# One stream for both stages of a bidirectional scan layer, with two changes of order, in a four-layer Trainium2 kernel

## The chip, the core and the metric

The kernel runs on one core of a Trainium2 chip. A core has five engines that run their own instruction queues and meet at semaphores: TensorE (PE, matmuls; its weight loads are listed as PEld), VectorE (DVE), ScalarE (ACT), GpSimd (POOL) and SyncE (SP, which here only issues DMA transfers). Each engine takes its instructions in program order. The metric is the device time of one execution in microseconds.

## The reference, cut to what matters

Four layers follow one another on an image batch of 8 x 64 x 64 x 64 in float32. Layer 1 and layer 3 are built on selective scans, and they are the ones that the change touches. Layer 3 is this:

```python
def mamba1(x, nw, ipw, cw, cb, xpw, dtw, dtb, Alog, Dp, opw):
    xn = rms_norm(x, nw)
    xz = xn @ ipw.T
    xc, z = (xz[..., :d], xz[..., d:])          # d = 256
    xc = silu(causal_dwconv(xc, cw, cb))
    dbl = xc @ xpw.T                            # 4 + 16 + 16 columns
    dt = softplus(dbl[..., :r] @ dtw.T + dtb)
    Bm, Cm = dbl[..., r:r + n], dbl[..., r + n:r + 2 * n]
    A = -exp(Alog)
    y = selective_scan(xc, dt, Bm, Cm, A)       # h = exp(dt A) h + dt x B;  y = sum_n h C
    y = (y + Dp * xc) * silu(z)
    return y @ opw.T

xt = mamba_bidir(xt, P, 0, 1) @ tlin_w + tlin_b + xt     # stage 0: along one image axis
xf = mamba_bidir(xf, P, 2, 3) @ flin_w + flin_b + xf     # stage 1: along the other axis
```

mamba_bidir runs mamba1 forward and on the reversed sequence with two sets of weights. A stage works on sequences of 64 positions, 16 states (n) and 256 channels (d). Stage 1 reads what stage 0 wrote, transposed. Layer 1 has the same recurrence in four directions with 128 channels.

## The kernel before, in words

**Tiles.** Layer 3 works in steps. A step is 8 sequences of 64 tokens in one direction: 512 tokens by 256 channels, held as tiles of 128 x 1024 (two halves of 128 channels side by side). Four groups g by two directions k are a chunk c of 8 steps, and 16 chunks (two per image, NB = 8 images) are a stage. So a stage has 128 steps of 16 states, 2048 scans.

**The stream** (`stream`, L433 to L579) is one loop over all the steps and states i of a stage. For each state, ACT makes `dA` = exp(dt A) (`decay`, L491), POOL makes `hb` = du B (`multiply_b`, L484), DVE runs the scan (L500), then DVE, or POOL for the "shared" states (5 or 4 of the 16), multiplies with C (`multiply_c`, L514), and PE adds the result into the accumulator `acc` with an identity matmul (`gather`, L306). The numbers `ahead` say how many states ahead the loads of B, the products hb and the loads of C are issued: (6, 3, 6) in layers 2 and 3, (5, 2, 3) in layer 1. In layer 3 (and 2) B and C of a state come as one tile `bc` and `fetch_c` does nothing. In layer 1 they come as two tiles from two pools of 4 (B) and 5 (C) buffers, and `fetch` (B) and `fetch_c` (C) both issue on SP's queue, B first (L543, L544). A load waits in that queue until its buffer is free: B's until POOL has made the hb that read it, C's until the product with C has been made.

**Beside the stream** run hand-ordered pieces. `prepare` of the next step is a generator of which one piece is taken per state: convolution and input projection on PE, Silu to `u`, a projection to dt, B and C (`dbl`), softplus to `dt` (L415), `du` = dt u on POOL (L2001), z's projection on PE (L2004), and then, on ACT, in this order: a copy that writes 1e30 into dt at one end of every sequence (L2015, so that exp(dt A) is 0 and the state starts anew), and z's Silu (L2017). The copy must come after POOL has read dt for du. `drain` (L2030) multiplies acc by z once a step's states are in. `finish` (L2046 to L2066) makes the output of a group: five matmuls, an ACT evacuation to `out`, and at an image's end (stage 0) or a chunk's end (stage 1) a store.

`begin` (L1884 to L1935) brings in a chunk. It loads `raw` twice (both 64-partition halves hold the same tokens, the lower one a position later), squares half of it at a time on ACT (L1900), averages on PE, copies the row to `ms` (L1906), sends it by DMA to `rs` spread over partitions (L1908), takes root and reciprocal, sends that to DRAM and back as `inv` in all partitions, and multiplies `xn` = raw inv on POOL (L1930). It is started by `done` of the first step of the chunk before, as a background task (`behind`) that advances one piece per state.

**Stages.** `layer3` calls `l3_stage` twice. Each call opens its own pools, issues 18 weight loads of its stage on SP, builds the products that the steps use (taps, w_z, w_end, w_res, skip, minus exp of A), clears raw and inv on POOL, runs `begin(0)` to its end, and then runs its own stream of 128 steps. `sq` is a tile of 64 x 1024 and `ms` one of 1 x 1024, each with one buffer. z's weights `w_z` lie in partitions 0 to 63.

Of the kernel before, what the change touches and what calls it, by code (L numbers as in the profile page):

```python
# [268 lines left out]
class Net:  # L269
# [163 lines left out]
    def stream(self, pools, ahead, steps, behind, rest=None):  # L433
# [1384 lines left out]
    def l3_stage(self, s, src, dst):  # L1818
# [5 lines left out]
        W, H = 512, 512 // HW  # L1824
        with ExitStack() as ctx:
            pool = lambda n, b, **k: ctx.enter_context(tc.tile_pool(name=f"l3{s}{n}", bufs=b, **k))
# [5 lines left out]
            def stage(name):  # L1832

                w = self.d["l3_" + name][:, 2 * s : 2 * s + 2]
                t = cp.tile(list(w.shape), F32, name="w_" + name)
                nc.sync.dma_start(t, w)
                return t

            linb = self.load(cp, "l3_linb")
            nw, w_in, cb, xp, dtw, dtb, A, D, w_out = (  # L1840
                stage(n) for n in ("nw", "in", "cb", "xp", "dtw", "dtb", "A", "D", "out")
            )
            lin = stage_lin = cp.tile([C, 2, C], F32, name="w_lin")
            nc.sync.dma_start(stage_lin, self.d["l3_lin"][:, s])
            self.minus_exp(A)
            nc.vector.tensor_scalar(A, A, -1e-27, None, ALU.min)
            skip = [self.diag(cp, f"skip{k}", D[:, k, :], 2) for k in range(2)]


            taps = [cp.tile([128, 2, 256], F32, name=f"taps{k}") for k in range(2)]  # L1850
            w_z = cp.tile([C, 2, 256], F32, name="w_z")
            w_end = cp.tile([128, 2, 2, C], F32, name="w_end")
            for k in range(2):
                for m in range(2):
                    for r in range(2):
                        row = self.d["l3_taps"][2 * s + k, m, r : r + 1, :]
                        nc.sync.dma_start(taps[k][r * C : r * C + C, m, :], row.to_broadcast([C, 256]))
                for m in range(2):
                    nc.vector.scalar_tensor_tensor(
                        taps[k][:, m, :], w_in[:, k, :256], nw[:, k : k + 1], taps[k][:, m, :], ALU.mult, ALU.mult  # L1860
                    )
                nc.vector.tensor_scalar(w_z[:, k, :], w_in[:C, k, 256:], nw[:C, k : k + 1], None, ALU.mult)

                for j in range(2):
                    ps = pp.tile([128, T], F32, name="mm")
                    nc.tensor.matmul(ps[:, :C], w_out[:, k, j * 128 : j * 128 + 128], lin[:, k, :], start=True, stop=True)
                    nc.scalar.copy(w_end[:, k, j, :], ps[:, :C])
            w_res = cp.tile([C, C], F32, name="w_res")
            nc.vector.tensor_tensor(w_res, lin[:, 0, :], lin[:, 1, :], ALU.add)
            nc.vector.tensor_tensor(w_res, w_res, self.ident[:C, :C], ALU.add)  # L1870
# [3 lines left out]
            nc.vector.memset(endless, 1e30)  # L1874

# [8 lines left out]
            def begin(c):  # L1884
# [4 lines left out]
                hold = chunks[c] = {"x": x}  # L1889
                from_ = src[q, rows, part * 4 * W : (part + 1) * 4 * W].rearrange("p (s t) -> p s t", t=HW)  # L1890
# [5 lines left out]
                for j in range(2):  # L1896
                    yield CALM_FREE
                    sq = p1.tile([C, T], F32, name="sq")
                    o = sq.rearrange("p (s t) -> p s t", t=HW)
                    nc.scalar.activation(o, x[:C, j * 2 * H : (j + 1) * 2 * H, ends[0]], AF.Square)  # L1900
# [4 lines left out]
                    ms = p1.tile([1, T], F32, name="ms")  # L1905
# [33 lines left out]
            class Step:  # L1939
# [6 lines left out]
                def __init__(self, c, g, k):  # L1946
                    self.c, self.g, self.k, self.rev = c, g, k, k == 1
                    self.shared = (2, 6, 10, 14) if k and g % 2 else (1, 4, 7, 10, 13)
                    self.lanes = [(slice(j * W, j * W + W), A[:, k, j, :]) for j in range(2)]

                def ready(self):

                    while begun.get(self.c) in behind:
                        net.advance(behind)

                def prepare(self):
                    k, hold = self.k, chunks[self.c]
# [6 lines left out]
                    for j in range(2):  # L1964
                        for m, f in enumerate((4, 6) if k else (3, 1)):
                            nc.tensor.matmul(  # L1966
                                tokens(px[:, j * W : j * W + W]),
                                taps[k][:, m, j * 128 : j * 128 + 128],
# [7 lines left out]
                    for j in range(2):  # L1976
                        at = slice(j * W, j * W + W)
                        nc.scalar.activation(u[:, at], px[:, at], AF.Silu, bias=cb[:, k, j : j + 1])  # L1978
                    pd = pp.tile([128, T], F32, name="mm")[:36, :W]
                    for j in range(2):  # L1980
                        nc.tensor.matmul(pd, xp[:, k, j, :], u[:, j * W : j * W + W], start=j == 0, stop=j == 1)  # L1981
# [7 lines left out]
                    for j in range(2):  # L1989
                        nc.tensor.matmul(  # L1990
                            pt[:, j * W : j * W + W], dtw[:, k, j * 128 : j * 128 + 128], dbl[0:4], start=True, stop=True
# [4 lines left out]
                    for j in range(2):  # L1996
                        at = slice(j * W, j * W + W)
                        net.softplus_act(dt[:, at], pt[:, at], dtb[:, k, j : j + 1])
# [13 lines left out]
                    yield CALM  # L2012

                    at = HW - 1 if k else 0
                    nc.scalar.copy(dt.rearrange("p (s t) -> p s t", t=HW)[:, :, at], endless)  # L2015
                    z = self.z = p2.tile([128, T], F32, name=f"z{k}")
                    nc.scalar.activation(z, pz, AF.Silu)  # L2017
# [5 lines left out]
                def skip(self, acc):  # L2023
                    for j in range(2):
                        at = slice(j * W, j * W + W)
                        nc.tensor.matmul(acc[:, at], skip[self.k][:, j, :], self.u[:, at], start=True, stop=False)
                    return True

                def drain(self, acc):
                    nc.vector.tensor_tensor(self.z, acc, self.z, ALU.mult)  # L2030
                    chunks[self.c][f"y{self.k}"] = self.z

                def done(self):
                    c, g = self.c, self.g
# [6 lines left out]
            def finish(c, g, ys):  # L2041
# [3 lines left out]
                x = chunks[c]["x"][:C, g * H : g * H + H, ends[0]]  # L2045
                nc.tensor.matmul(ps.rearrange("p (s t) -> p s t", t=HW), w_res, x, start=True, stop=False)  # L2046
                for k in range(2):
                    for j in range(2):
                        nc.tensor.matmul(  # L2049
                            ps, w_end[:, k, j, :], ys[k][:, j * W : j * W + W], start=False, stop=k == 1 and j == 1  # L2050
# [5 lines left out]
                if first:  # L2056
                    images[b] = p1.tile([C, L if s == 0 else 4 * W], F32, name="out")
# [10 lines left out]
            net = self  # L2068
# [30 lines left out]
```

## Time and profile before

| | us |
|---|---|
| timed runs, median of 3 | 24834.52 |
| timed runs, lowest to highest | 24824.01 to 24847.65 |
| profiled execution | 24819.55 |
| its span, first to last instruction | 24817.8 |

The profile is that of one execution. It reports for each engine when it was busy, and what released it where it waited. Over the span PE is busy 85%, DVE 90%, ACT 60% and POOL 89%, at a mean granted clock of TensorE of 0.940. The layers lie one after another in it:

| stretch, from the timeline | us |
|---|---|
| layer 1, first to last load of B for its stream | 1223.1 to 8458.4 |
| layer 2, first to last load of B and C for its scan | 8947.7 to 10596.2 |
| layer 3, first load to first scan's start | 11453.2 to 11520.9 |
| stage 0, first to last scan's start | 11520.9 to 18122.4 |
| stage 1, first to last scan's start | 18202.5 to 24800.8 |

The durations of the instructions that matter, from the page's groups: hb 2.36 us on POOL (L484), the scan 2.28 us on DVE (L500), the product with C 1.22 us on DVE and 2.36 us on POOL (L514), dA 0.69 us per half on ACT (L491), a switch of ACT's function table 1.28 us. "Idle before <-X" names the instruction that ended an engine's wait.

### The profile page before, as it was taken

To read this page: it belongs to the slowest core of one execution; us is meant where nothing else is said; L and a number is where in the kernel's file an instruction comes from. 1 tells how busy PE (TensorE), PEld (TensorE's weight loads), DVE (VectorE), ACT (ScalarE), POOL (GpSimd) and SP (SyncE) were. 2 spreads that over 40 slices of the span, in tenths; PEclk is the share of its full clock that TensorE was granted. 3 is DMA by queue.
4 is the path that set the end of the run, shared out by engine and by line. 5 is a ranking of instruction groups with operands and counts; after the bars stand their busy time and mean duration, and the time that the engine had idled before them with its cause. 6 is when DMAs were issued, how large, how long until landed. Compare 5 with 4: busy or idle time off the path is not lost. (4 is left out here: it accounts for less than half of the span.)

```text
span 24817.8 us, 193238 instructions
## 1 busy us (share of the span) xinstructions
PE 21209.1 (85%) x53146; PEld 8277.5 (33%) x53146; DVE 22437.6 (90%) x12958; ACT 14770.8 (60%) x18827; POOL 22097.5 (89%) x10583
## 2 busy tenths in 40 slices
PE   8877888888888888888888888888878888888888
PEld 6522333333333323322333333333323333333333
DVE  5399999999999679978999999999989999999999
ACT  4355555555555456624666666666666666666666
POOL 0199999999999669977999999999989999999999
PEclk9889999999999999999999999999989999999999
DMA  2399899899889669933455555555545554555454
GB/s 65 88 324 326 310 320 319 310 319 318 313 315 317 225 224 344 339 87 98 168 172 169 173 169 171 169 173 170 168 156 173 168 173 167 173 168 174 168 173 158
DMA packets 1835374, 5282.70 MB, mean 213 GB/s; under 512 B 533792, under 2 KB 540004, under 8 KB 1831984
## 3 DMA queue, kind: packets, MB, share of 16 engines
q1 hardware_dynamic: 1809712, 5207.00, 61.9%
q10 hardware_dynamic: 24576, 63.33, 0.7%
q8 instruction: 423, 6.93, 0.1%
q14 instruction: 663, 5.43, 0.1%
HBM read 5112.85 MB, written 156.11 MB: 212 GB/s over the span
## 5 line engine op out<-in xcount | busy, mean ns | idle before, releaser
L484 POOL TENSOR_TENSOR hb<-du,bc 128x1024 f32<-128x1024 f32 x4608 | 10745.6, 2359 | 201.3 <-DVE h L500 142.5
L306 PE MATMUL acc<-hc,ident 128*128 128x512 f32 x18560 | 8793.2, 615 | 109.8 <-DVE img L1266 61.4
L491 ACT ACTIVATE dA<-dt,w_A 128x512 f32<-128x512 f32 x8192 | 5655.4, 691 | 3950.7 <-DVE hc L514 2884.6
L500 DVE TENSOR_TENSOR_SCAN dA<-dA,hb 128x1024 f32<-128x1024 f32 x3320 | 7578.5, 2283 | 227.9 <-ACT dA L491 151.0
L306 PE MATMUL acc<-h,ident 128*128 128x512 f32 x8064 | 4623.7, 702 | 2390.1 <-POOL h L514 2361.7
L306 PEld LDWEIGHTS acc<-hc,ident 128*128 128x128 f32 x18560 | 3641.3, 200 | 5245.3 <-issue 4558.1
L484 POOL TENSOR_TENSOR hb<-du,b 128x1024 f32<-128x1024 f32 x2048 | 4837.5, 2395 | 460.4 <-DVE dA L500 220.7
L514 DVE TENSOR_TENSOR hc<-dA,bc 128x1024 f32<-128x1024 f32 x3232 | 3956.3, 1224 | 245.6 <-issue 5.8
L491 ACT ACTIVATE dA<-dt,w_l_A 128x1024 f32<-128x1024 f32 x2560 | 2857.1, 1117 | 1002.4 <-DVE hc L514 762.6
L500 DVE TENSOR_TENSOR_SCAN h<-dA,hb 128x1024 f32<-128x1024 f32 x1416 | 3229.2, 2280 | 148.2 <-ACT dA L491 144.8
L306 PEld LDWEIGHTS acc<-h,ident 128*128 128x128 f32 x8064 | 1560.4, 211 | 5100.2 <-POOL h L514 3403.4
L514 POOL TENSOR_TENSOR h<-h,bc 128x1024 f32<-128x1024 f32 x1376 | 3242.3, 2356 | 14.2 <-DVE h L500 14.2
L500 DVE TENSOR_TENSOR_SCAN dA<-dA,carry,hb 128x1024 f32<-128x1024 f32 x1320 | 3093.1, 2343 | 83.2 <-ACT dA L491 31.1
L514 DVE TENSOR_TENSOR hc<-dA,c 128x1024 f32<-128x1024 f32 x1408 | 1723.5, 1224 | 141.9 <-DMA c<-bc 32.0
L514 POOL TENSOR_TENSOR h<-h,c 128x1024 f32<-128x1024 f32 x640 | 1521.6, 2378 | 9.5 <-ACT carry L1249 8.9
L491 ACT ACT_TABLE_LOAD x1126 | 1444.7, 1283 | 20.0
L500 DVE TENSOR_TENSOR_SCAN h<-dA,carry,hb 128x1024 f32<-128x1024 f32 x600 | 1404.5, 2341 | 31.8 <-ACT dA L491 22.0
L1249 ACT COPY carry<-dA 128x1 f32<-128x1 f32 x1056 | 167.6, 159 | 1675.2 <-DVE hc L514 1635.5
L1966 PE MATMUL mm<-xn,taps 128*128 128x512 f32 x2048 | 939.1, 600 | 34.3 <-POOL xn L1930 31.1
L721 POOL MEMSET xf<- 128x24 f32 x33 | 4.3, 142 | 857.0 <-PE ps L742 728.0
L2001 POOL TENSOR_TENSOR du<-dt,u 128x1024 f32<-128x1024 f32 x256 | 602.8, 2355 | 18.5 <-ACT dt L415 18.5
L1981 PE MATMUL mm<-u,w_xp 128*36 128x512 f32 x1024 | 489.8, 601 | 149.2 <-ACT u L1978 140.1
(320 smaller groups left out, 18515.0 us busy)
## 6 DMA issues: line engine op xcount, KB each, us to landing
bc<-bc SPq DMA_DIRECT2D x4096, 512.0 KB
b<-bc SPq DMA_DIRECT2D x2048, 512.0 KB
c<-bc SPq DMA_DIRECT2D x2048, 512.0 KB
bc<-bc SPq DMA_DIRECT2D x512, 1024.0 KB
tmp<-rs SPq DMA_DIRECT2D x93, 512.0 KB
raw<-x SPq DMA_DIRECT2D x64, 512.0 KB
inv<-rs SPq DMA_DIRECT2D x64, 512.0 KB
tmp<-x SPq DMA_DIRECT2D x192, 128.0 KB
```

The source lines that it names most:

```text
L306: self.nc.tensor.matmul(o, lhsT, r, start=start, stop=stop)
L484: nc.gpsimd.tensor_tensor(s.shaped(hb[i]), s.shaped(s.du), B.pop(i), ALU.mult)
L491: nc.scalar.activation(dA[i][:, cut], s.dt[:, cut], AF.Exp, scale=A[:, n : n + 1])
L500: nc.vector.tensor_tensor_scan(h[:, way], dA[i][:, way], hb.pop(i)[:, way], s.first(n), ALU.mult, ALU.add)
L514: engine.tensor_tensor(s.shaped(o), s.shaped(h), CC.pop(i), ALU.mult)
L721: nc.gpsimd.memset(x[:, :, HW:], 0.0)
L1249: nc.scalar.copy(self.carry[:, n : n + 1], h[:, last : last + 1])
L1966: nc.tensor.matmul(tokens(px[:, j * W : j * W + W]), taps[k][:, m, j * 128 : j * 128 + 128], xn[:, :, f : f + HW], start=m == 0, stop=m == 1,)
L1981: nc.tensor.matmul(pd, xp[:, k, j, :], u[:, j * W : j * W + W], start=j == 0, stop=j == 1)
L2001: nc.gpsimd.tensor_tensor(du, dt, u, ALU.mult)
```

## The change

Three edits, cut to their core. The first is in `stream` and takes effect where B and C have their own pools, that is in layer 1:

```diff
             need(i + ahead[1], "du")
+            fetch_c(i + ahead[2])
             fetch(i + ahead[0])
-            fetch_c(i + ahead[2])
             multiply_b(i + ahead[1])
```

The second is at the end of `prepare`, with the weights of z now in partitions 64 to 127:

```diff
                         nc.tensor.matmul(
                             tokens(pz[:, j * W : j * W + W]),
-                            w_z[:, k, j * 128 : j * 128 + 128],
-                            xn[:C, :, 3 : 3 + HW],
+                            w.z[:, k, j * 128 : j * 128 + 128],
+                            xn[C:, :, 4 : 4 + HW],
...
                     yield CALM
+                    z = self.z = p2.tile([128, T], F32, name=f"z{k}")
+                    nc.scalar.activation(z, pz, AF.Silu)
 
                     at = HW - 1 if k else 0
                     nc.scalar.copy(dt.rearrange("p (s t) -> p s t", t=HW)[:, :, at], endless)
-                    z = self.z = p2.tile([128, T], F32, name=f"z{k}")
-                    nc.scalar.activation(z, pz, AF.Silu)
```

The third makes `layer3` one function with one set of pools. A class `Weights` holds a stage's weights; `load` issues its 18 loads (in this order: out, lin, nw, in, 8 of taps, cb, xp, dtw, dtb, A, D), of which w_in, w_out and lin go into two buffers of the stream's pool `bc` (they are read only while building), and `build` makes the products. Steps, chunks and `finish` carry the stage s as well, and read their weights from `weights[s]`, their input from `srcs[s]` and their output from `dsts[s]`:

```diff
     def layer3(self, src, dst):
-        self.l3_stage(0, src, self.hbm["x4"])
-        self.l3_stage(1, self.hbm["x4"], dst)
+        srcs, dsts = (src, self.hbm["x4"]), (self.hbm["x4"], dst)
...
+                def load(self):
+                    spare = pools[0].tile([128, 2, W], F32, name="bc")
+                    self.w_in = pools[0].tile([128, 2, W], F32, name="bc")
+                    self.w_out = self.take("out", spare[:C, 0, :].rearrange("p (k t) -> p k t", k=2))
+                    self.lin = spare[:C, 1, : 2 * C].rearrange("p (k t) -> p k t", k=2)
+                    nc.sync.dma_start(self.lin, net.d["l3_lin"][:, s])
+                    self.nw = self.take("nw")
+                    self.take("in", self.w_in)
...
                 for j in range(2):
                     yield CALM_FREE
-                    sq = p1.tile([C, T], F32, name="sq")
+                    both = p1.tile([128, T], F32, name="sq")
+                    sq, ms = both[:C], both[C : C + 1]
...
                     if self.k == 1:
-                        net.urgent.append(Task(finish(c, g, [chunks[c]["y0"], chunks[c]["y1"]])))
-                    if self.k == 0 and g == 0 and c + 1 < 2 * NB:
-                        begun[c + 1] = Task(begin(c + 1))
-                        behind.append(begun[c + 1])
+                        net.urgent.append(Task(finish(self.s, self.c, self.g, [hold["y0"], hold["y1"]])))
+                    more = self.s * 2 * NB + self.c + 1
+                    if self.k == 0 and self.g == 0 and more < 4 * NB:
+                        at = divmod(more, 2 * NB)
+                        begun[at] = Task(begin(*at))
+                        behind.append(begun[at])
...
             with tc.manual_schedule():
-                Task(begin(0)).run()
-                steps = [Step(c, g, k) for c in range(2 * NB) for g in range(4) for k in range(2)]
+                first = Task(begin(0, 0))
+                first.step()
+                weights[0].load()
+                weights[0].build()
+                first.run()
+                weights[1].load()
+                weights[1].build()
+                steps = [
+                    Step(s, c, g, k) for s in range(2) for c in range(2 * NB) for g in range(4) for k in range(2)
+                ]
                 self.stream(pools, (6, 3, 6), steps, behind)
```

In `build`, the four products for w_end go into one PSUM tile with one copy, where there were four of each; the rest is the same work per stage, now once for each stage before the one stream. `first.step()` issues the loads of raw for the first chunk ahead of the weights. What the last stage does at its end is as before.

More of the change, by code (lines that the diff above doesn't have):

```diff
@@ L1814, in layer3 @@
     def layer3(self, src, dst):
-        self.l3_stage(0, src, self.hbm["x4"])
-        self.l3_stage(1, self.hbm["x4"], dst)
-    def l3_stage(self, s, src, dst):
         nc, tc = self.nc, self.tc
         W, H = 512, 512 // HW
+        srcs, dsts = (src, self.hbm["x4"]), (self.hbm["x4"], dst)
         with ExitStack() as ctx:
-            pool = lambda n, b, **k: ctx.enter_context(tc.tile_pool(name=f"l3{s}{n}", bufs=b, **k))
+            pool = lambda n, b, **k: ctx.enter_context(tc.tile_pool(name="l3" + n, bufs=b, **k))
             cp, p1, p2 = pool("c", 1), pool("p1", 1), pool("p2", 2)
@@ L1830, in l3_stage @@
             hp = pool("h3", 3, space=DRAM)
[L1832 to L1837, printed above, removed]
-            linb = self.load(cp, "l3_linb")
[L1840 to L1870, printed above, removed]
+            linb = self.load(cp, "l3_linb")
             mean = cp.tile([C, 1], F32, name="mean")
@@ L1874, in l3_stage, with __init__, take, build @@
             nc.vector.memset(endless, 1e30)
+            class Weights:
+                def __init__(self, s):
+                    self.s = s
+                def take(self, name, t=None):
+                    w = net.d["l3_" + name][:, 2 * self.s : 2 * self.s + 2]
+                    if t is None:
+                        t = cp.tile(list(w.shape), F32, name=f"w_{name}{self.s}")
+                    nc.sync.dma_start(t, w)
+                    return t
+                def load(self):
+                    s = self.s
+                    spare = pools[0].tile([128, 2, W], F32, name="bc")
[5 more added lines that the diff above has]
+                    self.take("in", self.w_in)
+                    self.taps = [cp.tile([128, 2, 256], F32, name=f"taps{s}{k}") for k in range(2)]
+                    for k in range(2):
+                        for m in range(2):
+                            for r in range(2):
+                                row = net.d["l3_taps"][2 * s + k, m, r : r + 1, :]
+                                nc.sync.dma_start(self.taps[k][r * C : r * C + C, m, :], row.to_broadcast([C, 256]))
+                    self.cb, self.xp = self.take("cb"), self.take("xp")
+                    both = cp.tile([128, 2, 256], F32, name=f"both{s}")
+                    self.dtw, self.z = self.take("dtw", both[:4]), both[C:]
+                    self.dtb, self.A, self.D = self.take("dtb"), self.take("A"), self.take("D")
+                def build(self):
+                    s = self.s
+                    ps = pools[5].tile([128, T], F32, name="acc")[:, : 4 * C]
+                    for i in range(4):
+                        k, j = divmod(i, 2)
+                        nc.tensor.matmul(
+                            ps[:, i * C : i * C + C],
+                            self.w_out[:, k, j * 128 : j * 128 + 128],
+                            self.lin[:, k, :],
+                            start=True,
+                            stop=True,
+                        )
+                    self.end = cp.tile([128, 2, 2, C], F32, name=f"w_end{s}")
+                    nc.scalar.copy(self.end.rearrange("p k j o -> p (k j o)"), ps)
+                    for k in range(2):
+                        for m in range(2):
+                            nc.vector.scalar_tensor_tensor(
+                                self.taps[k][:, m, :],
+                                self.w_in[:, k, :256],
+                                self.nw[:, k : k + 1],
+                                self.taps[k][:, m, :],
+                                ALU.mult,
+                                ALU.mult,
+                            )
+                    for k in range(2):
+                        nc.vector.tensor_scalar(
+                            self.z[:, k, :], self.w_in[C:, k, 256:], self.nw[C:, k : k + 1], None, ALU.mult
+                        )
+                    net.minus_exp(self.A)
+                    nc.vector.tensor_scalar(self.A, self.A, -1e-27, None, ALU.min)
+                    self.res = cp.tile([C, C], F32, name=f"w_res{s}")
+                    nc.vector.tensor_tensor(self.res, self.lin[:, 0, :], self.lin[:, 1, :], ALU.add)
+                    nc.vector.tensor_tensor(self.res, self.res, net.ident[:C, :C], ALU.add)
+                    self.skip = [net.diag(cp, f"skip{s}{k}", self.D[:, k, :], 2) for k in range(2)]
@@ L1876, in l3_stage @@
+            net = self
+            weights = [Weights(s) for s in range(2)]
             raw = [cp.tile([128, 4 * H, HW + 6], F32, name=f"raw{j}") for j in range(2)]
@@ L1882, in l3_stage, with begin @@
             chunks = {}
-            def begin(c):
+            def begin(s, c):
                 b, part = divmod(c, 2)
@@ L1888, in begin @@
                 x = raw[c % 2]
-                hold = chunks[c] = {"x": x}
-                from_ = src[q, rows, part * 4 * W : (part + 1) * 4 * W].rearrange("p (s t) -> p s t", t=HW)
+                hold = chunks[s, c] = {"x": x}
+                from_ = srcs[s][q, rows, part * 4 * W : (part + 1) * 4 * W].rearrange("p (s t) -> p s t", t=HW)
                 for r in range(2):
@@ L1904, in begin @@
                     yield CALM
-                    ms = p1.tile([1, T], F32, name="ms")
                     nc.scalar.copy(ms, ps[:1, :])
@@ L1944, in l3_stage, with __init__ @@
                 spread = staticmethod(lambda t, m: t[:, m : m + 1, :].to_broadcast([128, 2, W]))
-                def __init__(self, c, g, k):
-                    self.c, self.g, self.k, self.rev = c, g, k, k == 1
+                def __init__(self, s, c, g, k):
+                    self.s, self.c, self.g, self.k, self.rev = s, c, g, k, k == 1
+                    self.w = weights[s]
                     self.shared = (2, 6, 10, 14) if k and g % 2 else (1, 4, 7, 10, 13)
-                    self.lanes = [(slice(j * W, j * W + W), A[:, k, j, :]) for j in range(2)]
+                    self.lanes = [(slice(j * W, j * W + W), self.w.A[:, k, j, :]) for j in range(2)]
                 def ready(self):
-                    while begun.get(self.c) in behind:
+                    while begun.get((self.s, self.c)) in behind:
                         net.advance(behind)
                 def prepare(self):
-                    k, hold = self.k, chunks[self.c]
+                    k, w, hold = self.k, self.w, chunks[self.s, self.c]
                     xn = hold["xn"][:, self.g * H : self.g * H + H, :]
@@ L1967, in prepare @@
                                 tokens(px[:, j * W : j * W + W]),
-                                taps[k][:, m, j * 128 : j * 128 + 128],
+                                w.taps[k][:, m, j * 128 : j * 128 + 128],
                                 xn[:, :, f : f + HW],
@@ L1977, in prepare @@
                         at = slice(j * W, j * W + W)
-                        nc.scalar.activation(u[:, at], px[:, at], AF.Silu, bias=cb[:, k, j : j + 1])
+                        nc.scalar.activation(u[:, at], px[:, at], AF.Silu, bias=w.cb[:, k, j : j + 1])
                     pd = pp.tile([128, T], F32, name="mm")[:36, :W]
                     for j in range(2):
-                        nc.tensor.matmul(pd, xp[:, k, j, :], u[:, j * W : j * W + W], start=j == 0, stop=j == 1)
+                        nc.tensor.matmul(pd, w.xp[:, k, j, :], u[:, j * W : j * W + W], start=j == 0, stop=j == 1)
                     yield True
@@ L1990, in prepare @@
                         nc.tensor.matmul(
-                            pt[:, j * W : j * W + W], dtw[:, k, j * 128 : j * 128 + 128], dbl[0:4], start=True, stop=True
+                            pt[:, j * W : j * W + W], w.dtw[:, k, j * 128 : j * 128 + 128], dbl[0:4], start=True, stop=True
                         )
@@ L1997, in prepare @@
                         at = slice(j * W, j * W + W)
-                        net.softplus_act(dt[:, at], pt[:, at], dtb[:, k, j : j + 1])
+                        net.softplus_act(dt[:, at], pt[:, at], w.dtb[:, k, j : j + 1])
                     yield
@@ L2025, in skip @@
                         at = slice(j * W, j * W + W)
-                        nc.tensor.matmul(acc[:, at], skip[self.k][:, j, :], self.u[:, at], start=True, stop=False)
+                        nc.tensor.matmul(acc[:, at], self.w.skip[self.k][:, j, :], self.u[:, at], start=True, stop=False)
                     return True
@@ L2030, in drain, with finish @@
                     nc.vector.tensor_tensor(self.z, acc, self.z, ALU.mult)
-                    chunks[self.c][f"y{self.k}"] = self.z
+                    chunks[self.s, self.c][f"y{self.k}"] = self.z
                 def done(self):
-                    c, g = self.c, self.g
+                    hold = chunks[self.s, self.c]
                     if self.k == 1:
-                        net.urgent.append(Task(finish(c, g, [chunks[c]["y0"], chunks[c]["y1"]])))
-                    if self.k == 0 and g == 0 and c + 1 < 2 * NB:
-                        begun[c + 1] = Task(begin(c + 1))
-                        behind.append(begun[c + 1])
-            def finish(c, g, ys):
+                        net.urgent.append(Task(finish(self.s, self.c, self.g, [hold["y0"], hold["y1"]])))
[4 more added lines that the diff above has]
+                        behind.append(begun[at])
+            def finish(s, c, g, ys):
+                w, dst = weights[s], dsts[s]
                 b, part = divmod(c, 2)
@@ L2044, in finish @@
                 ps = pp.tile([128, T], F32, name="mm")[:C, :W]
-                x = chunks[c]["x"][:C, g * H : g * H + H, ends[0]]
-                nc.tensor.matmul(ps.rearrange("p (s t) -> p s t", t=HW), w_res, x, start=True, stop=False)
+                x = chunks[s, c]["x"][:C, g * H : g * H + H, ends[0]]
+                nc.tensor.matmul(ps.rearrange("p (s t) -> p s t", t=HW), w.res, x, start=True, stop=False)
                 for k in range(2):
@@ L2049, in finish @@
                         nc.tensor.matmul(
-                            ps, w_end[:, k, j, :], ys[k][:, j * W : j * W + W], start=False, stop=k == 1 and j == 1
+                            ps, w.end[:, k, j, :], ys[k][:, j * W : j * W + W], start=False, stop=k == 1 and j == 1
                         )
@@ L2056, in finish @@
                 if first:
-                    images[b] = p1.tile([C, L if s == 0 else 4 * W], F32, name="out")
+                    images[b] = p1.tile([C, L], F32, name="out")
+                    if s == 1:
+                        images[b] = images[b][:, : 4 * W]
                 f = (part * 4 + g) * H
@@ L2066, in finish @@
                     nc.sync.dma_start(dst[q, rows] if s == 0 else dst[q, rows, part * 4 * W : (part + 1) * 4 * W], images[b])
-            net = self
             with tc.manual_schedule():
-                Task(begin(0)).run()
-                steps = [Step(c, g, k) for c in range(2 * NB) for g in range(4) for k in range(2)]
+                first = Task(begin(0, 0))
[8 more added lines that the diff above has]
+                ]
                 self.stream(pools, (6, 3, 6), steps, behind)
```

## The prediction

> **What bounds the kernel.** I read the slices of the page first: from the twentieth of the forty on, VectorE (DVE) and GpSimd (POOL) show 9 throughout, except in the thirtieth, where both fall to 8. Cutting the span at the two ends of that dip gives (engine columns in the header's order):
>
> ```profile
> core 0: us, PE busy (x) PEld busy (x) DVE busy (x) ACT busy (x) POOL busy (x), PEclk, DMA share, GB/s
> 11521.00:18125.00 6604.00, 5711.49 (x11983) 2172.28 (x11981) 6408.67 (x3630) 4477.43 (x5898) 6511.36 (x2841) 0.95 0.51 170
> 18125.00:18202.00 77.00, 34.53 (x57) 11.15 (x58) 6.41 (x18) 18.55 (x26) 17.86 (x10) 0.61 0.45 94
> 18202.00:24801.00 6599.00, 5708.04 (x11981) 2171.66 (x11980) 6406.17 (x3629) 4448.88 (x5899) 6509.55 (x2841) 0.95 0.51 170
> ```
>
> Rows 1 and 3 are layer 3's stages. POOL is busy 98.6%, DVE 97.0%, with only issue gaps between its instructions: both are full. Row 2 is the seam, 77 us with almost nothing on either. The timeline says what fills it:
>
> ```profile
> 18134.49 0.52 SPq L2066 DMA_DIRECT2D x<-out  x1
> ...
> 18179.58 5.33 POOL L1930 TENSOR_TENSOR xn<-raw,inv 128x560 f32<-128x560 f32 x4 [39.28 <-DMA inv<-rs]
> ...
> 18202.53 2.30 DVE L500 TENSOR_TENSOR_SCAN dA<-dA,hb 128x1024 f32<-128x1024 f32 x1 [33.67 <-ACT dA L491]
> ```
>
> The last image is stored, 18 weight loads and the first chunk's load go out one after another, its norm (begin) runs alone, then the first step's prepare runs alone. The stream restarts 80 us after its last scan (18122.39).
>
> **Part 1, one stream over both stages.** First scans of consecutive chunks (8 steps) are 412.7 to 413.3 us apart in both stages; the pair across the seam (17717.6 to 18202.5) is 485.0 apart. In one stream that chunk is like any other, since begin of stage 1's chunk 0 becomes a background task that starts seven steps earlier, and the image of x4 it reads was stored some thirteen chunks before: **485.0 - 413.0 = -72.0 us**. POOL gives the same by another way: from its last hb (ends 18116.8) to its first of stage 1 (18197.6) are 80.8 us, of which 10.0 (one h, one du, four xn) remain work: 70.8.
>
> What the start of layer 3 pays instead (first scan 11520.9, nothing beside it):
> - Stage 0's weights. Before: 18 loads, then raw, which lands for the first Square at 11474.4. After: raw first, then the loads, then Exp of A on ScalarE (ACT) ahead of that Square. Eighteen loads took 11453.7 to 11468.4 with one store among them, 0.77 us each; raw (two loads of 512 KB) is now in front. I put A's landing at 11474.2, Square at 11475: +0.7.
> - sq and ms now share one single-buffered tile, so the second Square waits for the DMA that reads the first ms: issued 11480.14, landed 11481.9 by the landing events, where Square began at 11480.0: +1.9.
> - Stage 1's weights go into the SP queue behind inv, whose transfers (DMA share 0.87) land at 11498.9; Exp of A1 (the 17th load) stands on ACT before the first u Silu (11505.55). Here a rule of the Trainium skill ("DMA: Bandwidth & Descriptors", Anatomy of one DMA) bears: about 2 us fixed cost per DMA. Paid one by one, 18 loads would be 36 us, 25 exposed. The row has 0.77 us each, as the waits overlap; ten loads remain behind inv's landing, A1 lands near 11507 plus the 2.6 above. The rule that speaks against this edit is in "ScalarE: Activation LUTs", table sets: batch functions by set. Exp between the norm's Sqrt and Silu puts a switch into the exposed chain. The skill prices it at 2.66 us with its drain, an estimate of +2.7; the trace has the load at 1.28 us and the activation 0.02 later, so 1.3. I take the row. Both together: u about 3.4 us later than the +2.6.
> Sum +6; least 0 (all hidden in the idle chain), most +25 (the serial price).
>
> The shared tile also stands in all 31 later chunks. There the landing comes 0.5 to 2.3 us after the present start of the second Square, but ACT idles after it:
>
> ```profile
> 18310.02 1.06 ACT L1900 ACTIVATE sq<-raw 64x1024 f32<-64x1024 f32 x1
> 18313.80 1.42 ACT L491 ACTIVATE dA<-dt,w_A 128x512 f32<-128x512 f32 x2 [2.71 <-DVE hc L514]
> ```
>
> 2.7 us of cover, so 0 (if the wait outgrows it, each us queues dA and then the scan: 31 us per us). The moved z weights, same matmul shape, 0.
>
> **Part 2, ends behind z's Silu.** Twice a chunk ACT waits with the copy at L2015 for du on POOL and Silu and dA queue behind it:
>
> ```profile
> 13051.61 2.40 POOL L2001 TENSOR_TENSOR du<-dt,u 128x1024 f32<-128x1024 f32 x1
> ...
> 13054.05 0.22 ACT L2015 COPY dt<-endless 128x16 f32<-128x16 f32 x1 [2.33 <-POOL du L2001]
> ...
> 13059.43 2.29 DVE L500 TENSOR_TENSOR_SCAN h<-dA,hb 128x1024 f32<-128x1024 f32 x1 [2.14 <-ACT dA L491]
> ```
>
> After the change table load and Silu (2.3 us) fill the wait, so dA starts 2.3 us earlier and the DVE stall goes; its twin one step later (1.6) too. DVE's gaps at that place of its order (over 0.15 us) sum to 51 us per stage, 102 in all. Is it on the path? POOL idles only 5.2 us per chunk (83 per stage), always for a buffer that DVE frees, in the chunk's later steps. From 13350 to 13554 it is never idle, and both stalls of the next chunk (13472, 13524) lie in that stretch; it ends here:
>
> ```profile
> 13532.91 2.34 POOL L514 TENSOR_TENSOR h<-h,bc 128x1024 f32<-128x1024 f32 x1
> ...
> 13535.31 3.78 PE L306 MATMUL acc<-h,ident 128*128 128x512 f32 x4 [3.29 <-POOL h L514]
> ...
> 13538.88 4.69 PE L306 MATMUL acc<-hc,ident 128*128 128x512 f32 x8
> ...
> 13543.61 1.23 DVE L2030 TENSOR_TENSOR z<-acc,z 128x1024 f32<-128x1024 f32 x1 [0.56 <-PE acc L306]
> ...
> 13558.46 2.35 POOL L484 TENSOR_TENSOR hb<-du,bc 128x1024 f32<-128x1024 f32 x1 [2.05 <-DVE h L500]
> ```
>
> POOL's last h feeds TensorE (PE), and z's drain on DVE already waits 0.56 us for it: DVE has caught up with POOL although it stalled 3.7 us on the way. Without the stalls it waits about 4 us at z and at hb, POOL's time stands, and so does everything after z. **So 0 for the stream**, -0.6 at the exposed start (copy and du no longer in series). Bounds: 0 and -102.
>
> **Part 3, C's load ahead of B's.** Only layer 1 has separate B and C pools. Its waits (1500 to 8400 us):
>
> ```profile
> DVE hc L514 <- DMA c<-bc: 28.0, 18, 3.4
> ...
> POOL hb L484 <- DMA b<-bc: 19.3, 11, 3.4
> ...
> SPq L1239 <- POOL h L514: 983.9, 527, 2.0
> ```
>
> C waits where SP had been held by a tokens load and then let B and C out together: C's transfer follows B's by about 1.3 us (landings). Swapped, ten such events (0.6 to 2.5 us, 15.4 in sum) lose up to 1.3 each, about 12; at six of them B (n = 14), late as well, loses 1.3 more on POOL, of which I charge the whole, 8. The price elsewhere: the third row. C(i+3) waits for POOL's h(i-2), which comes after the hb that frees B(i+5); that wait now holds B too, 5 times in 16. Landing to use of B is 2.6 to 9.0 us (tenth to ninetieth percentile), and for the loads that would be held longest (n = 8 and 11) the tenth percentile is 4.3 and 6.5 against a hold of at most 2.7: hidden. Net **-4 us**, bounds -28 (all C waits) and +20 (B's waits double).
>
> **Sum**: -72 + 6 - 1 - 4 = **-71 us**. The profiled execution took 24819.6 us for a span of 24817.8, so 24749 by the same clock; the three timed runs have their median 15 us higher, 24834.5, and I forecast there: **24764 us**, -0.29%. A change under 0.2% (50 us) counts as none.
>
> **Rivals.**
> - z's Silu pays in full: DVE, not POOL, is the bound throughout. For: DVE stalls for nothing else there, and POOL's idle 166 us leaves room. Against: z's wait of 0.5 to 0.6 us in every chunk. 24764 - 102 = 24662.
> - The shared sq tile eats part of the seam: the landing grows beyond 2.7 us, as SP delivers that DMA behind a bc load waiting for its buffer. Against: 2.3 was the longest. It sits in the stretch where DVE leads, so it would count in full; with 1 us each, 24764 + 31 = 24795.
> - Slower: C holds B in layer 1. 527 holds lie ahead of B; the gain of 71 is gone at 71/527 = 0.13 us of POOL stall per hold. At 0.3 us: 24764 + 158 = 24922. For it: POOL's lead over the scan is near zero at n = 9, 11 and 14. Against: the slack above.
> - The seam does not close, if a wait on x4 or on a weights buffer keeps begin from running ahead: 24764 + 72 = 24836. Against: nothing it reads is late. Only a sliver.
>
> **How the numbers follow.** Forecast 0.70 (24745 to 24785, nearly all beyond 0.2%), z 0.12, shared tile 0.10, C holds B 0.06, seam 0.02. Faster: 0.68 + 0.12 = 0.80; same 0.15 (tile, seam, the forecast's edge, part of C); slower 0.05. Part of z's gain could come through, so the range goes down to 24690, leaving most of that case out, and up to 24800.
>
> **What would show it.** No dip in the slices; equal chunk pitch of 413 us across the seam; first scan of layer 3 some 6 us later after the end of layer 2. L2015's wait for du nearly gone, ACT no longer DVE's releaser there, but z's wait on PE up from 0.5 to about 4 us in one step of eight: if instead the pitch falls to 410, I am wrong about POOL. In layer 1, waits on c fall from 28 to about 16, waits on b rise by some 10; b's far higher means the slower rival.

## The result and the profile after

| | before | after |
|---|---|---|
| timed runs, median (9 each) | 24845.46 us | 24773.71 us |
| lowest to highest | 24824.01 to 24850.98 us | 24756.76 to 24779.39 us |
| profiled span | 24817.8 us | 24763.3 us |
| layer 3, first load to first scan | 67.8 us | 73.0 us |
| layer 3, first to last scan's start | 13279.9 us | 13208.9 us |
| chunk across the seam | 485.0 us | 413.0 us |
| mean of the other chunks but the first | 413.0 us | 413.0 us |

The ratio of the runs is 0.9971, with a 95% interval of 0.9963 to 0.998: 0.29% faster, 72 us of the median, clear of no change. The dip is gone from the page's 40 slices. Their rows for the two engines that bound layer 3 were, before,

```profile
DVE  5399999999999679978999999999989999999999
...
POOL 0199999999999669977999999999989999999999
```

and are now

```profile
DVE  5399999999999779978999999999999999999999
...
POOL 0199999999999669977999999999999999999999
```

Here are three stretches of the execution after, with the columns of the table in the prediction; the middle one is 77 us around the place where the stages meet:

```profile
11537.00:18117.00 6580.00, 5696.20 (x11962) 2167.30 (x11961) 6382.84 (x3615) 4484.57 (x5894) 6496.33 (x2837) 0.95 0.53 170
18117.00:18194.00 77.00, 67.91 (x142) 26.09 (x141) 75.67 (x43) 54.23 (x71) 74.51 (x33) 0.93 0.54 173
18194.00:24746.00 6552.00, 5675.40 (x11910) 2160.14 (x11909) 6362.89 (x3604) 4423.45 (x5855) 6461.92 (x2820) 0.95 0.53 170
```

DVE has 75.7 us of work in that stretch where it had 6.4. In this table the seam can no longer be found.

The second edit did what it says. ACT's own timeline in a step that used to wait for du has the table load and Silu first and then the copy, with no idle time:

```profile
13068.68 1.28 ACT L2052 ACT_TABLE_LOAD   x1
13069.97 1.02 ACT L2052 ACTIVATE z<-mm 128x1024 f32<-128x1024 f32 x1
13070.97 0.22 ACT L2056 COPY dt<-endless 128x16 f32<-128x16 f32 x1
13071.21 1.28 ACT L491 ACT_TABLE_LOAD   x1
```

ACT's waits for du in the copy, 116 us before, are no longer listed. Before, DVE had two stalls at that place in a chunk, of 2.14 us (in the prediction) and of 1.60, and z's drain at the end of the stretch waited little:

```profile
13111.57 2.29 DVE L500 TENSOR_TENSOR_SCAN h<-dA,hb 128x1024 f32<-128x1024 f32 x1 [1.60 <-ACT dA L491]
...
13130.64 1.23 DVE L2030 TENSOR_TENSOR z<-acc,z 128x1024 f32<-128x1024 f32 x1 [0.51 <-PE acc L306]
```

Now the largest wait for dA left in the stretch is one of 0.51 us. But the chunk is as long as before, and z's drain waits 2.45 us (the drain one step earlier 0.87, where it had waited for nothing):

```profile
13117.33 2.29 DVE L500 TENSOR_TENSOR_SCAN h<-dA,hb 128x1024 f32<-128x1024 f32 x1 [0.51 <-ACT dA L491]
...
13147.65 1.22 DVE L2069 TENSOR_TENSOR z<-acc,z 128x1024 f32<-128x1024 f32 x1 [2.45 <-PE acc L306]
```

In layer 1 (1500 to 8400 us) the two waits for loads changed places, and SP's wait for POOL's h grew. These lines answer to the three of before:

```profile
DVE hc L514 <- DMA c<-bc: 3.0, 5, 1.1
...
POOL hb L484 <- DMA b<-bc: 55.2, 56, 4.3
...
SPq L1239 <- POOL h L514: 1540.8, 512, 7.3
```

In this one execution layer 1's scans took 7263.3 us from first to last, 19 more than before, and POOL's hb there took 2.476 us where it had 2.395. Whether that belongs to the edit is the first question for the experiments.

### The profile page after: what moved, and what is told of

The parts are those of the page before. It is cut to its first block, busy times and chain, and to the rows that moved or that the text cites. A ratio compares the mean times of both kernels' runs of the same rounds, so it can differ in the third digit from the quotient of the medians.

```text
span 24763.3 us, 192937 instructions
## 1 busy us (share of the span) xinstructions
PE 21205.6 (86%) x53146; PEld 8272.3 (33%) x53146; DVE 22452.5 (91%) x12956; ACT 14796.2 (60%) x18824; POOL 22125.0 (89%) x10580
## 5 line engine op out<-in xcount | busy, mean ns | idle before, releaser
L484 POOL TENSOR_TENSOR hb<-du,b 128x1024 f32<-128x1024 f32 x2048 | 4919.7, 2476 | 467.4 <-DVE dA L500 205.6
```

Of the source, the lines that this page charges most:

```text
L484: nc.gpsimd.tensor_tensor(s.shaped(hb[i]), s.shaped(s.du), B.pop(i), ALU.mult)
```

## Experiments

Ratios are to the kernel before, run beside each group of experiments on the same chip. Pitch is the mean time between first scans of chunks, without the first chunk and the one across the seam. A lighter step is one with four shared states instead of five: POOL makes one product less in it, and DVE one more. Two steps of a chunk are lighter; in the kernels before and after these are g = 1 and 3, k = 1. "Ends before Silu" means that z's edit is undone.

| run | median us | ratio (95%) | pitch us |
|---|---|---|---|
| C in front, alone | 24830.06 | 1.0002 (0.9993 to 1.001) | 413.00 |
| all but C in front | 24763.49 | 0.9974 (0.9965 to 0.9984) | 413.02 |
| z's Silu first, alone | 24826.58 | 1.0000 (0.9992 to 1.0009) | 412.98 |
| all but z's Silu first | 24763.25 | 0.9975 (0.9965 to 0.9984) | 413.02 |
| sq and ms shared, alone (one execution) | 24828.96 | none | 412.98 |
| lighter steps g = 2, 3, k = 0 | 24754.51 | 0.9971 (0.9959 to 0.9982) | 412.46 |
| the same, ends before Silu | 24776.69 | 0.9982 (0.9975 to 0.9989) | 413.56 |
| lighter steps g = 1, 2, k = 1 | 24706.91 | 0.9955 (0.9941 to 0.9968) | 411.38 |
| the same, ends before Silu | 24717.88 | 0.9948 (0.9935 to 0.996) | 410.99 |
| g = 1, 2, k = 1, states 1, 5, 9, 13 | 24674.14 | 0.9928 (0.9916 to 0.994) | 409.66 |
| g = 2, 3, k = 0, states 1, 5, 9, 13 | 24793.7 | 0.9979 (0.9971 to 0.9987) | 413.71 |

**C's load, alone and undone.** Into the kernel before:

```diff
-            fetch(i + ahead[0])
             fetch_c(i + ahead[2])
+            fetch(i + ahead[0])
```

> The kernel before with C's load in front of B's as its only change. The recorded forecast (C gains a little): ratio 0.9998, layer 1's stream some 4 us shorter. The rival, read from the changed kernel's trace (waits of hb on B's load 19 to 55 us, hb in layer 1 2.395 to 2.476 us, first to last load of B 7235 to 7254 us): C in front costs 10 to 20 us, ratio 1.0004 to 1.0008, with waits on C near 3 us and on B near 55 us. If hb stays at 2.40 us here, its slowdown belongs to that one execution and not to the edit.

and the reverse in the changed kernel:

> The changed kernel with B's load in front of C's again. Forecast of the record: 4 us slower than the changed kernel. Rival: 10 to 20 us faster than it, ratio to before about 0.9965, layer 1's first to last load of B back near 7235 us.

Measured: 1.0002 and 0.9974, and neither tells the order from no change. Alone, the waits move as in the changed kernel: POOL's list in layer 1 has

```profile
POOL hb L484 <- DMA b<-bc: 49.8, 59, 4.0
```

and DVE's waits for C fall from 28.0 us to 1.6. But DVE's waits for POOL's hb there rise from 22.4 us to 49.7, so what C gave is taken back by B. The time from B's landing to its use falls from a median of 5.3 us to 3.4, that of C rises from 6.1 to 7.4. But hb takes 2.392 us here, and layer 1's scans take 7255.6 us. The three executions with C in front have 7263.3, 7255.6 and 7245.2 us, the ten with B in front, before and the further runs below, 7244.3 to 7269.7. The third run with C in front has hb at 2.392 us as well. So the slow hb does not come with the edit, and the 19 us lie within the scatter of layer 1. A gain or cost of some 10 us is below what these runs can tell.

**z's Silu, alone and undone.** Into the kernel before:

```diff
+                    z = self.z = p2.tile([128, T], F32, name=f"z{k}")
+                    nc.scalar.activation(z, pz, AF.Silu)
                     at = HW - 1 if k else 0
                     nc.scalar.copy(dt.rearrange("p (s t) -> p s t", t=HW)[:, :, at], endless)
-                    z = self.z = p2.tile([128, T], F32, name=f"z{k}")
-                    nc.scalar.activation(z, pz, AF.Silu)
```

> The kernel before with z's Silu ahead of the ends of sequences as its only change. Theory (POOL sets the time of the stretch in which ACT waits for du): ratio 1.0000 within 0.0003, chunk pitch 413.0 us, waits of the copy for du gone, z's wait on PE up from 41 to about 97 us over both stages. Rival (those DVE stalls are on the path): 102 us faster, ratio 0.9959, pitch 409.8 us.

> The changed kernel with the ends of sequences ahead of z's Silu again. Theory: same time as the changed kernel within 5 us, pitch 413.0 us, first scan of layer 3 0.6 us or more later after its first load. Rival: 100 us slower than the changed kernel, i.e. slower than before.

Measured: 1.0000, and 0.9975 against 0.9971 of the changed kernel; the pitch is 413.0 in all four. DVE's waits over layer 3 (11540 to 24700 us), of before and then of the run with this edit alone:

```profile
DVE h L500 <- ACT dA L491: 120.1, 91, 2.2
DVE dA L500 <- ACT dA L491: 42.4, 32, 33.7
DVE z L2030 <- PE acc L306: 40.7, 58, 2.8
```

```profile
DVE z L2030 <- PE acc L306: 89.7, 85, 2.8
DVE h L500 <- ACT dA L491: 61.5, 60, 2.2
DVE dA L500 <- POOL hb L484: 36.6, 13, 33.8
```

(The 33.7 and 33.8 are single waits at the second stage's start.) Some 59 us leave h's wait for dA, and 49 arrive at z. That is the exchange that the prediction drew, at half its size: DVE reaches POOL's front earlier and waits there. The rival's pitch of 409.8 is refuted.

**sq and ms in one tile**, alone, in the kernel before:

```diff
-                    sq = p1.tile([C, T], F32, name="sq")
+                    both = p1.tile([128, T], F32, name="sq")
+                    sq, ms = both[:C], both[C : C + 1]
...
-                    ms = p1.tile([1, T], F32, name="ms")
```

> The kernel before with sq and ms in one tile of one buffer as its only change. Theory: the second Square of each chunk waits 0.5 to 2.3 us for the DMA, inside 2.7 us of ACT's idle time; pitch 413.0 us in both stages, first scan of each stage 1.9 us later after its loads. Rival: the wait reaches DVE, pitch 413.5 to 415 us.

Measured: pitch 412.98, so the rival's 413.5 to 415 is refuted. At layer 3's start the second Square comes 7.64 us after the first instead of 5.64. The first scan comes 2.2 us later after the first load, but that total does not tell: in the run with C's load alone, which changes nothing in layer 3, it comes 1.6 us later too. In the changed kernel the wait is a line of ACT's list over layer 3:

```profile
ACT sq L1938 <- DMA rs<-sq: 21.9, 31, 2.3
```

That is 31 waits, one per chunk, 2.3 us at most, inside the 2.7 us of cover.

**Moving POOL's load, to test that POOL and DVE take turns.** In the changed kernel both engines have less than 408 us of work per chunk, the short gaps between instructions included (413.0 less 5.2 us of waits on POOL and 5.4 on DVE). The waits lie apart in its trace: POOL waits 2.1 us a chunk in each of the two lighter steps and at most 0.8 in any other, and DVE has 4.3 of its 5.4 us in the last two steps, behind the four pieces of xn that POOL makes from the end of the fourth step to the start of the seventh. If POOL sets the time where xn is made and DVE elsewhere, then the 413 is not a floor, and moving one product per step from the one stretch to the other must shorten it. These runs are built on the changed kernel with B in front:

```diff
-                    self.shared = (2, 6, 10, 14) if k and g % 2 else (1, 4, 7, 10, 13)
+                    self.shared = (2, 6, 10, 14) if not k and g >= 2 else (1, 4, 7, 10, 13)
```

> The changed kernel with B's load first, and in layer 3 the lighter set of shared states (4 products on POOL instead of 5) moved from the steps g = 1 and 3, k = 1 to the steps g = 2 and 3, k = 0, in which the next chunk's xn loads POOL. The sum of both engines' work over a chunk is unchanged. Theory (POOL and DVE take turns as the bound, each with about 407.4 us of work per chunk, and the 5 to 6 us above it are waits of one for the other): pitch falls from 413.0 to 408 to 410 us, ratio to before 0.993 to 0.9945. Rival (something else sets 413, such as PE or ACT): pitch stays at 413, ratio 0.997.

> As the run with the moved shared set, but with the ends of sequences ahead of z's Silu. Theory: where POOL no longer lags, either du is early and ACT waits little, so both agree within 0.3 us of pitch, or the waits remain and now stand on the path, up to 3.2 us of pitch (102 us). Rival (z's Silu is worth nothing under any balance): equal within 0.1 us of pitch.

Measured: 412.5 and 413.6. The expected gain of 3 to 5 us did not come. Two new waits stand in each chunk. ACT waits some 5 us at `out` for finish's matmuls (186 us over the stream), and z waits, as DVE's timeline of the first run has it:

```profile
13305.43 1.22 DVE L2069 TENSOR_TENSOR z<-acc,z 128x1024 f32<-128x1024 f32 x1 [5.15 <-PE acc L306]
```

The difference of 1.1 us between the two runs refutes the rival and lies in the range of the theory, but not by its cause: without the reorder ACT waits for du only 3.1 us in the whole stream. What makes the difference is open. The other choice of steps:

```diff
-                    self.shared = (2, 6, 10, 14) if k and g % 2 else (1, 4, 7, 10, 13)
+                    self.shared = (2, 6, 10, 14) if k and g in (1, 2) else (1, 4, 7, 10, 13)
```

> As the first of these runs, but the lighter set at the steps g = 1 and 2, k = 1: only one of the two stands in the stretch in which xn loads POOL. Theory: half to two thirds of the gain, pitch 409.5 to 411.5 us. Rival as there: 413.

> The balanced version that ran 411.6 us of pitch (lighter set at g = 1 and 2, k = 1), with the ends of sequences ahead of z's Silu. Theory (z's Silu is worth nothing only while POOL sets the stretch in which ACT waits for du; where POOL has been relieved there, the DVE stalls stand on the path): pitch 0.5 to 2 us longer, 16 to 60 us of time. Rival (worth nothing anywhere): the same within 0.1 us of pitch.

Measured: 411.4 (the later expectations write 411.6), in the range given, and 24706.91 us. So 413 was no floor set by PE or ACT: the same work, with one product placed otherwise, takes less. My theory of z fell in the second run: with the old order the pitch is 411.0, shorter, not longer, and not equal either, as the rival had it. There ACT waits 21.9 us for du in all, at most 0.6 at a time, where it had waited 116, so there was little left to gain. DVE's waits at h for dA are 13.8 us against 2.1, its waits at z 86 against 113. Why z waits more behind the new order is open.

In this arrangement z waits 113 us for PE. The next edit moves all four of the lighter steps' products on POOL one state earlier, the last one with them:

```diff
-                    self.shared = (2, 6, 10, 14) if k and g in (1, 2) else (1, 4, 7, 10, 13)
+                    self.shared = (1, 5, 9, 13) if k and g in (1, 2) else (1, 4, 7, 10, 13)
```

> That balanced version with the lighter steps' set at states 1, 5, 9, 13 instead of 2, 6, 10, 14, so that POOL's last product of such a step comes one state earlier. Theory (what is left above the 407 us of work per chunk is z's wait on PE for POOL's last product, 113 us over the stream): the wait falls and the pitch with it, to 410 to 411 us. Rival: 411.6 as before.

Measured: 409.66, 24674.14 us, 0.9928. Its interval lies below that of the changed kernel (0.9963 to 0.998), so this version beats both kernels. DVE's and POOL's first lines over the stream (11560 to 24600 us), before the edit (two lines of each run's two lists, DVE first):

```profile
DVE z L2069 <- PE acc L306: 112.9, 85, 3.9
...
POOL hb L484 <- DVE h L500: 85.4, 109, 2.1
```

and with it:

```profile
DVE z L2069 <- PE acc L306: 57.3, 57, 2.6
...
POOL hb L484 <- DVE h L500: 66.5, 118, 1.2
```

The waits named fall on both engines (DVE's waits for dA rise, from 12 us to 28), and the 1.7 us of pitch times 32 chunks make 55 us. That the last of the four products does it is not shown, since all four moved. The same set in the arrangement that had not worked:

> The arrangement that left the pitch at 413.0 (lighter set at g = 2 and 3, k = 0), with states 1, 5, 9, 13. There z waited up to 5.3 us for PE and ACT up to 5.3 us for the output's matmuls. Theory (those waits come from a last product at state 14 on POOL): both shrink, pitch 410 to 411.5 us. Rival: 413.0.

Measured: 413.7, where the same arrangement had 412.5 (not 413.0) without the set; z still waits up to 5.6 us, and ACT at `out` up to 3.6. So the last product's state alone is not what spoils that arrangement, and what does is open.

## Why the prediction was right, point by point

The forecast was 24764 us, 71 us less; the median is 24773.71, 72 us less. It lies 10 us above the forecast because the median of before rose by 11 us from three runs to nine. The interval of the ratio is some 21 us to each side, so the agreement to 1 us is luck. The terms as measured give -71.0 in the stream and +5.3 at its start, -66 in all, which lies in the interval too.

- **The seam** (-72.0). The pitch across it is 413.0 us: -72.0, as said. Both runs with the one stream and one of the two orders undone have 0.9974 and 0.9975, both runs with one order alone have 1.0000 and 1.0002. The one stream alone was not run, but as far as these intervals tell (some 20 us) the whole gain is this edit.
- **The start of layer 3** (+6 - 1). Measured from the first load to the first scan: 67.8 to 73.0 us, +5.3. In ACT's timeline (first load at 11464.38):

```profile
11487.64 1.06 ACT L1938 ACTIVATE sq<-raw 64x1024 f32<-64x1024 f32 x1
...
11495.21 1.08 ACT L1938 ACTIVATE sq<-raw 64x1024 f32<-64x1024 f32 x1 [1.85 <-DMA rs<-sq]
...
11521.59 1.28 ACT L2016 ACT_TABLE_LOAD   x1
11522.88 1.26 ACT L2016 ACTIVATE u<-mm,w_cb 128x512 f32<-128x512 f32 x2
```

  The first Square comes 23.3 us after the first load where it came 21.2: +2.0, not +0.7, since Exp waits for A behind raw. The second waits 1.85 (said: 1.9). u comes 58.5 after it where it came 52.4: +6.1 (said: 3.4 beyond 2.6). The term of Square was too small by 1.3 us, and the one of A1 too large by about as much. Between u and the first scan 0.8 us come back, since Silu no longer stands behind the copy (said: 0.6). Silu's table load behind Exp takes the row's 1.28 us, and u follows 0.01 us later: 1.3, not 2.7. Eighteen loads one by one (+25) were not paid; the 2 us per load on which that bound rests are given by the Trainium skill ("DMA: Bandwidth & Descriptors", Anatomy of one DMA) for DMAs that GpSimd issues, while SP issues these.

  The split is that of one execution. Over all runs with the one stream the start takes 72.4 to 73.7 us, over the four without it 67.8 to 70.0, so its cost is some 2.5 to 6 us. The second Square's wait and, where Silu goes first, the gain behind u (u to scan 14.2 to 14.5 us, against 15.0 with the ends first) repeat in every one of them.
- **z's Silu** (0). Right in time and in mechanism, at half the size. The wait at z was to grow by 3.5 us in one step of eight, 112 us in all; it grew by 56, from 40.7. DVE's list over layer 3 (11540 to 24700 us) after:

```profile
DVE z L2069 <- PE acc L306: 96.8, 81, 3.2
DVE h L500 <- ACT dA L491: 54.5, 62, 2.2
```

  Only 66 us left h's wait for dA, since shorter waits came up on the way (in the chunk above 0.51 us); of these, 56 arrived at z and 5.5 at hb.
- **C in front** (-4). The exchange came, but both sizes were wrong, and so was the step that called the longer hold of B hidden. C's waits were to fall to 16 us and fell to 3; B's were to rise by 10 and rose by 36. I had counted only the events in which both loads were late, at 1.3 us each, and a hold of at most 2.7 us. In fact the order moved the whole queue: SP's waits for POOL's h last 3.0 us on average and up to 7.3 (before 1.9 and 2.0), the median slack of B's loads fell from 5.3 to 3.5 us, and POOL waited for 56 of them instead of 11. DVE's waits for hb rose from 22.4 to 59.5 us, more than the 25 us by which those for C fell. On the time this shows nothing: alone, the interval is -17 to +25 us. That the term came out near nothing all the same is luck.
- **The rivals.** The slower one had its mechanism (SP's wait for POOL's h, 984 to 1541 us), but 0.07 us more of POOL's wait per hold, (55.2 - 19.3) / 527, against the 0.13 from which it decides. The shared tile stayed within its cover by 0.4 us.
- The profiled executions differ by 54.5 us only: -71.0 in the stream, +5.3 at the start, and +11.2 in all that lies before layer 3's first load, where layer 1 had +19.0. One execution's layer 1 does not carry a verdict; the nine runs have 72.

## What to carry to other kernels

A gap that stands between two saturated stretches is worth its length less the work in it, and is best read from the distance of like instructions on both sides. A stall on one of two engines that are both almost full is worth nothing while the other one sets that stretch: look at whether the other is idle at that time, and at the next point where the stalled engine waits for it. Where two engines take turns as the bound, moving work between stretches at a constant sum can gain what removing single stalls does not: 3.4 us of 413 in the best of the arrangements here. In another it gained next to nothing (412.5 and 413.7), so each place has to be tried.

## What the runs showed of the hardware

POOL's hb in layer 1, the same instruction on tiles of the same size, ran at different levels from execution to execution, each kept through the whole layer: 2.391 to 2.395 us on average in seven executions, 2.413 to 2.416 in five, 2.476 in one. Layer 1's scans took 7244.3 to 7255.6 us from first to last in the seven and 7262.1 to 7269.7 in the other six. The level does not follow the order of the loads: C stands in front in two of the seven and in one of the six. The chip alone does not decide it either: of four executions on one chip, two ran at the first level and two at the second. The granted clocks are 0.939 to 0.941 in all thirteen. Layer 3's pitch held within 0.05 us over the seven executions that leave POOL's load in layer 3 as it was. No run here shows the cause of the levels. A difference of 20 us in one profile of this kernel is therefore no evidence for an edit.
